# Rows of the source slots: from PSUM to their tile's partitions within SBUF, in two parts of sources, in a graph network's three convolutions

## The chip, the cores and the metric

The kernel runs on one core of a Trainium2 chip. The metric is the time of one execution in device microseconds. The engines are named as the profile names them: PE (TensorE matmul; PEld its weight loads), DVE (VectorE), ACT (ScalarE), POOL (GpSimd), SP (SyncE, which only issues DMAs here). Sixteen DMA engines serve all queues; q1 is the queue of the DMAs that SP issues, q0 that of the gathers that POOL issues.

## The reference

A graph of 12500 nodes (128 features each) and 200000 edges, sorted by destination. The first layer is an attention over each node's incoming edges; the change hardly touches it. The second layer is three graph convolutions, each followed by a batch norm:

```python
def _gcn_norm(edge_index, n):
    loop = arange(n)
    src, dst = concat([edge_index[0], loop]), concat([edge_index[1], loop])
    deg = segment_sum(ones_like(dst), dst, n)
    dinv = rsqrt(deg)
    return src, dst, dinv[src] * dinv[dst]

def _gcn_conv(x, W, b):
    h = x @ W
    return segment_sum(h[src] * norm[:, None], dst, n) + b

h = _batch_norm(relu(_gcn_conv(x, W1, b1)), g1, beta1)     # 128 -> 256
h = _batch_norm(relu(_gcn_conv(h, W2, b2)), g2, beta2)     # 256 -> 128
h = _batch_norm(_gcn_conv(h, W3, b3), g3, beta3)           # 128 -> 128
```

All is in float32. On average 16 edges end at a node.

## The kernel before

**Tiles and slots.** Destinations are cut into 106 tiles of TN = 118 nodes, sources into NS = 98 groups of P = 128 nodes. For every tile and every source group there are SB = 13 slots, each of which holds one edge or none; a tile thus has SL = 98 x 13 = 1274 slots. Edges that find no slot (there are 19.3 per tile and group on average) are overflow, up to OV = 768 per tile in JO = 6 columns of 128. The slot lists are made once, by a sort on DVE that runs beside the attention (`place_edges`): gi_d in DRAM holds, for every slot, the source's number within its group (uint8), dlS in SBUF the destination's number within the tile, srcO the overflow's source rows. If the overflow doesn't fit, another path (`conv_rows`) is taken; with these inputs the slots' path (`conv_slots`) is.

**One convolution.** The table t_d (12544 rows of 512 B in DRAM) holds the transformed features, and hs the same in SBUF, as 98 groups of 128 rows. Tiles go in NBK = 12 blocks of TB = 9.

- `take(b, m)` fetches the slots' rows of a block: for seven stretches of SG = 14 source groups it loads gi (one list, broadcast to 128 partitions), DVE compares it with the partition's number (go, L1221, a one-hot matrix, four groups at a time), PE multiplies go with hs (gp, L1224: 117 slot rows of one group, 9 tiles x 13), ACT copies four groups from PSUM to stage (L1226), and SP writes stage to the DRAM tile m (L1228), in 112 and 5 partitions, 7168 B each.
- `reduce(b, m)` sums by tile: POOL gathers the overflow's rows from t_d (rows, L148, six DMAs of 128 rows), SP reads the tile's 1274 slot rows back from m as mr (L1245, RC = 10 rows per partition, 5120 B), DVE makes the one-hots of the destinations (oh, L1249, 16 columns of 118), and PE adds up in zp: the tile's own rows tg with the identity (L1159), ten matmuls of mr (L1253), six of rows (L1255). After GN = 3 tiles, `finish` multiplies by dinv (db, L1163), and `use` applies bias and relu on ACT.

The rows of take(b) are issued between the tiles of reduce(b - 1); the order on each engine is set by the Tile framework's scheduler from this program order, and tiles rotate over bufs buffers (gi 3, go 3, stage 2, mr 3, rows 5, oh 2; gp and zp two each in PSUM). Every engine, and SP as the queue of DMA issues, runs its instructions in order.

**Between convolutions.** The results stay in big (SBUF, 128 x 12544 float32); the first convolution has 256 outputs, and its second half goes to DRAM as hb_d. `transform` multiplies them with the next weights into hs and t_d.

The profile counts two matmul records for one float32 matmul.

## Time and profile before

| | us |
|---|---|
| median of three runs (lowest, highest) | 6156.63 (6151.24, 6157.75) |
| the profiled execution, its own time | 6154.56 |
| its span | 6152.8 |
| busy: PE / PEld / DVE / ACT / POOL | 4406.0 / 4115.5 / 3396.2 / 1011.7 / 4084.2 |
| attention and sort, from the start | 0 to 2957 |
| first convolution | 3008 to 4028 |
| transform | 4028 to 4091 |
| second convolution | 4091 to 5072 |
| transform | 5072 to 5113 |
| third convolution | 5113 to 6093 |
| last stage and end | 6093 to 6153 |

The stages' bounds are the first and the last matmul of a stage. A group of the profile has line, engine, operation, out<-in by the program's names, and how often it ran, then busy us and the mean ns of one, then the engine's idle time just before it and what ended most of that. L12 is line 12 of the kernel. "DMA share" is the busy share of the 16 DMA engines, "PEclk" the clock granted to PE.

### The profile page before, as it was taken

What the parts mean: (1) busy time and instruction counts of PE and PEld (TensorE: products, weight loads), DVE (VectorE), ACT (ScalarE), POOL (GpSimd) and SP (SyncE); (2) the same over time, 40 slices, a digit from 0 to 9 for tenths busy, and PEclk for the clock granted to TensorE, in tenths of its full rate; (3) what the DMA queues carried; (4) which work ended last, traced back from release to release, by engine and by line L of the source; (5) the groups of instructions that cost most, each with busy time, mean ns of one, the idle gap of its engine ahead of it and who ended that gap; (6) DMA issues with size and microseconds to landing.
All of it is one profiled execution on the core that took longest, in us unless ns stands there. A gap on an engine that the chain in (4) does not pass through costs nothing. (4 is left out here: it accounts for less than half of the span.)

```text
span 6152.8 us, 80384 instructions
## 1 busy us (share of the span) xinstructions
PE 4406.0 (72%) x28564; PEld 4115.5 (67%) x28564; DVE 3396.2 (55%) x5972; ACT 1011.7 (16%) x2374; POOL 4084.2 (66%) x3617
## 2 busy tenths in 40 slices
PE   6676666666666665767487787877787787778777
PEld 2666655555566665666377777777777776777777
DVE  7566688887876677655243343353343344434344
ACT  3111111110111111111112122111121211112120
POOL 0777788888888888777266566636666664666663
PEclk9677766666676776767788888898888888888888
DMA  6555544433444444454588888878888887888888
GB/s 188 152 143 138 137 112 106 113 103 109 105 128 120 122 112 112 131 132 114 150 214 216 218 216 218 213 209 217 219 216 221 213 211 204 219 219 219 221 215 209
DMA packets 607714, 1051.07 MB, mean 171 GB/s; under 512 B 191227, under 2 KB 418491, under 8 KB 607201
## 3 DMA queue, kind: packets, MB, share of 16 engines
q1 hardware_dynamic: 464311, 695.85, 41.5%
q0 software_dynamic: 142608, 348.39, 23.9%
q8 instruction: 232, 3.80, 0.3%
q14 instruction: 175, 1.43, 0.1%
q10 hardware_dynamic: 388, 1.60, 0.1%
HBM read 773.19 MB, written 272.26 MB: 170 GB/s over the span
## 5 line engine op out<-in xcount | busy, mean ns | idle before, releaser
L148 POOL DMA_INDIRECT rows<-t_d,srcO x1908 | 1827.6, 958 | 1329.2 <-issue 560.2
L148 POOL DMA_INDIRECT kv<-kv_d,srcA x1696 | 2252.3, 1328 | 536.7 <-issue 484.3
L1249 DVE TENSOR_TENSOR oh<-nums,dlS 128x1888 f32<-128x1888 f32 x318 | 674.3, 2121 | 1527.2 <-PE zp L1255 1517.9
L1253 PE MATMUL zp<-oh,mr 128*128 128x118 f32 x6360 | 966.6, 319 | 567.5 <-DMA mr<-m 440.4
L1253 PEld LDWEIGHTS zp<-oh,mr 128*128 128x128 f32 x6360 | 925.5, 233 | 586.4 <-DMA mr<-m 348.7
L1019 PE MATMUL qe<-qt,oht 128*128 128x128 f32 x3392 | 841.4, 415 | 247.3 <-DVE kv L1020 110.7
L1224 PE MATMUL gp<-hs,go 128*117 128x128 f32 x7056 | 891.8, 281 | 125.8 <-DVE go L1221 69.8
L1019 PEld LDWEIGHTS qe<-qt,oht 128*128 128x128 f32 x3392 | 767.1, 310 | 289.7 <-issue 166.8
L1224 PEld LDWEIGHTS gp<-hs,go 128*117 128x117 f32 x7056 | 831.9, 184 | 165.1 <-issue 117.1
L1226 ACT COPY stage<-gp 117x512 f32<-117x512 f32 x1008 | 521.8, 532 | 1375.0 <-PE gp L1224 936.8
L1020 DVE TENSOR_TENSOR kv<-qe,kv 128x512 f32<-128x512 f32 x424 | 289.4, 685 | 678.8 <-DMA kv<-kv_d,srcA 536.8
L1089 PE MATMUL acc<-vals,oh 128*118 128x137 f32 x3392 | 539.8, 329 | 150.5 <-DVE vals L1082 150.0
L1089 PEld LDWEIGHTS acc<-vals,oh 128*118 128x118 f32 x3392 | 522.1, 225 | 171.6 <-DVE vals L1082 171.3
L1221 DVE TENSOR_SCALAR go<-gi,iota_q 128x468 f32<-128x468 uint8 x1008 | 427.8, 456 | 224.5 <-DMA gi<-gi_d 111.8
L1255 PE MATMUL zp<-oh,rows 128*128 128x118 f32 x3816 | 513.2, 288 | 0.2 <-DMA rows<-t_d,srcO 0.2
L1255 PEld LDWEIGHTS zp<-oh,rows 128*128 128x128 f32 x3816 | 492.2, 206 | 0.4 <-DMA rows<-t_d,srcO 0.4
L1058 PE MATMUL ends<-ident,mg 128*8 128x128 f32 x212 | 53.0, 343 | 344.4 <-DVE mg L1053 305.6
L1082 DVE TENSOR_TENSOR vals<-kv,vals 128x2048 f32<-128x2048 f32 x106 | 242.3, 2286 | 27.2 <-ACT vals L1081 26.8
L1058 PEld LDWEIGHTS ends<-ident,mg 128*8 128x8 f32 x212 | 11.7, 96 | 366.1 <-DVE mg L1053 298.8
L1023 DVE TENSOR_REDUCE sc<-kv 128x128 f32<-128x2048 f32 x106 | 240.8, 2272 | 0.0
L677 DVE TENSOR_TENSOR oh<-iota_f,dlA 128x1888 f32<-128x1888 f32 x106 | 224.0, 2113 | 5.0 <-PE acc L1089 5.0
L1036 PE MATMUL sm<-wbd,et 128*128 128x32 f32 x848 | 167.8, 351 | 45.0 <-DVE mg L1075 37.7
(242 smaller groups left out, 3648.1 us busy)
## 6 DMA issues: line engine op xcount, KB each, us to landing
m<-stage SPq DMA_DIRECT2D x252, 784.0 KB
mr<-m SPq DMA_DIRECT2D x318, 560.0 KB
dw_b<-dlb_d SPq DMA_DIRECT2D x106, 512.0 KB
gi<-gi_d SPq DMA_DIRECT2D x252, 204.8 KB
rows<-t_d,srcO POOLq DMA_INDIRECT x1908
kv<-kv_d,srcA POOLq DMA_INDIRECT x1696
ebx<-in_edge_attr_dram SPq DMA_DIRECT2D x106, 256.0 KB
mr<-m SPq DMA_DIRECT2D x318, 75.0 KB
```

The lines of the kernel that those rows point to most:

```text
L148: nc.gpsimd.indirect_dma_start(out=o, out_offset=None, in_=table[:, :], in_offset=bass.IndirectOffsetOnAxis(ap=idx, axis=0))
L1019: nc.tensor.matmul(qe[:, k, :], ohv[:, :, j + k], qt, start=True, stop=True)
L1020: nc.vector.tensor_tensor(qk[:, j:j + 4, :], qe, qk[:, j:j + 4, :], op=ALU.mult)
L1023: nc.vector.tensor_reduce(sc.rearrange("p h j -> p j h"), qk.rearrange("p j (h c) -> p j h c", h=H), AX.X, ALU.add)
L1082: nc.vector.tensor_tensor(vh[:, :, :, :C], kv[:, :, D:].rearrange("p j (h c) -> p j h c", h=H), vh[:, :, :, C:].to_broadcast([P, JJ, H, C] ...
L1089: nc.tensor.matmul(acc, oh[:, j, :], va[:, j, :], start=(j == 0), stop=(j == JJ - 1))
L1221: nc.vector.tensor_scalar(go[:, :n], gv[:, a:a + n], iota_q, None, op0=ALU.is_equal)
L1224: nc.tensor.matmul(gp[:, i, :], go[:, i].rearrange("p t k -> p (t k)"), hs[:, g * SG + a + i, :], start=True, stop=True)
L1226: nc.scalar.copy(stage[:, a:a + n, :], gp[:, :n, :])
L1249: nc.vector.tensor_tensor(oh, nums.unsqueeze(1).to_broadcast(sh), dlS[:, t, :].unsqueeze(2).to_broadcast(sh), op=ALU.is_equal)
L1253: nc.tensor.matmul(zp[:, i, :], mr[:q, j, :], oh[:q, j, :], start=False, stop=False)
L1255: nc.tensor.matmul(zp[:, i, :], rows[:, j, :], oh[:, RC + j, :], start=False, stop=(j == JO - 1))
```

## The change

The slots' rows no longer pass through DRAM. A block has TB = 8 tiles with SB = 16 slots each, so that one matmul of go and hs yields 128 slot rows, ordered slot by slot (k, then the tile t). The destination tile mr in SBUF has the shape (128, 8 tiles, 7, 128), and SP copies stage to it by SBUF-to-SBUF DMAs: the row group (k, t) of stage goes to the partitions q x 16 + k, at tile t, for the seven (or six) source groups at once. A transfer reads 128 partitions and writes 16.

Because mr now holds a whole block, the sources are cut into two parts, 8 x 7 = 56 groups and 7 x 6 = 42 groups. `take(b, part, mr)` fills mr for one part in four batches of up to 14 groups (eight transfers of 458,752 B for part 0, seven of 393,216 B for part 1), between the tiles of the part before. The sums of a tile stay open over both parts: `add_first` adds part 0 (seven matmuls), `add_rest` own rows, part 1 (six) and overflow (four). A matmul with zeros opens the PSUM bank of four tiles, and `finish` comes after four tiles (NG = 4) in place of three. There are 14 blocks, and 512 overflow edges per tile in four columns. dlS is set to -1 first, since not all its places are written. go reads gi in the order slot, tile, so neighbouring elements stand a tile's slots apart.

Buffers: gi 2, go 3, stage 2, mr 2, rows 6, oh 2; in PSUM gp 2, zp 3, hq 2. big and the DRAM tile m are gone. The results of every convolution go to DRAM (h_d), and transform and the last stage read them from there. The lists gi_d are laid out by batch, eight DMAs per block.

```diff
 MG = 4
-SB = 13
-OV = 768
+SB = 16
+OV = 512
 JO = OV // P
 TB = P // SB
-GN = 3
-SG = 14
+CA, CB = 7, 6
 NOT = 1 << 23
...
+    NA = TB * CA
+    NQ = (NS - NA) // CB
+    assert NA + NQ * CB == NS and NQ <= TB
+    parts = [(0, CA, TB), (NA, CB, NQ)]
+    RC = CA + CB
+
+    batches = [[(0, q, 2) for q in range(0, TB, 2)], [(1, q, min(2, NQ - q)) for q in range(0, NQ, 2)]]
+    MB = 2 * CA
...
-    gi_d = dram.tile([NBK, NS // SG, TB, SG * SB], U8, name="gi_d")
-    hb_d = dram.tile([P, NP], FP, name="hb_d")
+    gi_d = dram.tile([NBK, TB * SL], U8, name="gi_d")
+    h_d = [dram.tile([P, NP], FP, name=f"h{i}_d") for i in range(2)]
...
+        def batch(b, part, q, m):
+            s0, n, _ = parts[part]
+            s0, n = s0 + q * n, n * m
+            return s0, n, gi_d[b, TB * SB * s0:TB * SB * (s0 + n)].rearrange("(t k) -> t k", t=TB)
...
             for b in range(NBK):
                 tn = min(TB, NTT - b * TB)
-                nc.sync.dma_start(gi_d[b, :, :tn, :].rearrange("g t k -> t g k"),
-                                  sl[b * TB:b * TB + tn, :].rearrange("t (g k) -> t g k", g=NS // SG))
-            if NTT % TB:
-                none = rt.tile([NS // SG, (TB - NTT % TB) * SG * SB], U8, name="none")
-                yield
-                nc.vector.memset(none, 255)
-                nc.sync.dma_start(gi_d[NBK - 1, :, NTT % TB:, :].rearrange("g t k -> g (t k)"), none)
+                for x in batches[0] + batches[1]:
+                    s0, n, gi = batch(b, *x)
+                    nc.sync.dma_start(gi[:tn], sl[b * TB:b * TB + tn, s0 * SB:(s0 + n) * SB])
...
+                gy, gx, sg, mt, ga, ohs, wk = (pool(n, b) for n, b in (("gy", 2), ("gx", 3), ("sg", 2), ("mt", 2),
+                                                                         ("ga", 6), ("ohs", 2), ("wk", 2)))
...
-                def take(b, m):
-                    for g in range(NS // SG):
-                        stage = sg.tile([TS, SG, D], FP, name="stage")
-                        gi = gy.tile([P, TB, SG * SB], U8, name="gi")
-                        nc.sync.dma_start(gi.rearrange("p t k -> p (t k)"),
-                                          gi_d[b, g].rearrange("t k -> (t k)").unsqueeze(0)
-                                          .to_broadcast([P, TS * SG]))
-                        gv = gi.rearrange("p t (s k) -> p s t k", k=SB)
-                        for a, n in groups(SG, 4):
-                            go = gx.tile([P, 4, TB, SB], FP, name="go")
-                            nc.vector.tensor_scalar(go[:, :n], gv[:, a:a + n], iota_q, None, op0=ALU.is_equal)
-                            gp = ps.tile([TS, 4, D], FP, name="gp")
-                            for i in range(n):
-                                nc.tensor.matmul(gp[:, i, :], go[:, i].rearrange("p t k -> p (t k)"),
-                                                 hs[:, g * SG + a + i, :], start=True, stop=True)
-                            nc.scalar.copy(stage[:, a:a + n, :], gp[:, :n, :])
-                        for x, y in ((0, 112), (112, TS)):
-                            nc.sync.dma_start(m[x:y, g * SG:(g + 1) * SG, :], stage[x:y])
...
+                def ones_at(dl):
+                    oh = ohs.tile([P, CB + JO, TN], FP, name="oh")
+                    sh = [P, dl.shape[1], TN]
+                    nc.vector.tensor_tensor(oh[:, :sh[1]], nums.unsqueeze(1).to_broadcast(sh),
+                                            dl.unsqueeze(2).to_broadcast(sh), op=ALU.is_equal)
+                    return oh
+
+                def take(b, part, mr):
+                    n = parts[part][1]
+                    for _, q, m in batches[part]:
+                        s0, w, slots = batch(b, part, q, m)
+                        gi = gy.tile([P, P * MB], U8, name="gi")
+                        nc.sync.dma_start(gi[:, :P * w], slots.rearrange("t k -> (t k)").unsqueeze(0)
+                                          .to_broadcast([P, P * w]))
+                        gv = gi[:, :P * w].rearrange("p (t s k) -> p s k t", t=TB, k=SB)
+                        stage = sg.tile([P, MB, D], FP, name="stage")
+                        for a, c in groups(w, 4):
+                            go = gx.tile([P, 4, SB, TB], FP, name="go")
+                            nc.vector.tensor_scalar(go[:, :c], gv[:, a:a + c], iota_q, None, op0=ALU.is_equal)
+                            gp = pg.tile([P, 4, D], FP, name="gp")
+                            for i in range(c):
+                                nc.tensor.matmul(gp[:, i, :], go[:, i].rearrange("p k t -> p (k t)"),
+                                                 hs[:, s0 + a + i, :], start=True, stop=True)
+                            nc.scalar.copy(stage[:, a:a + c, :], gp[:, :c, :])
+                        for i in range(m):
+                            nc.sync.dma_start(mr[(q + i) * SB:(q + i + 1) * SB, :, :n, :],
+                                              stage[:, i * n:(i + 1) * n, :])
                         yield
 
-                def reduce(b, m):
-                    for t0 in range(b * TB, min(NTT, (b + 1) * TB), GN):
-                        n = min(GN, NTT - t0)
-                        zp = ps.tile([P, GN, TN], FP, name="zp")
-
-                        def add(i):
-                            t = t0 + i
+                zps = {}
+
+                def add_first(b, mr):
+                    for t in range(b * TB, min(NTT, (b + 1) * TB)):
+                        if t % NG == 0:
+                            zps[t // NG] = pz.tile([P, NG, TN], FP, name="zp")
+                            nc.tensor.matmul(zps[t // NG].rearrange("p a b -> p (a b)"), zero[:, :P], zero,
+                                             start=True, stop=False)
+                        zp = zps[t // NG][:, t % NG, :]
+                        oh = ones_at(dlS[:, t, :CA])
+                        for j in range(CA):
+                            nc.tensor.matmul(zp, mr[:, t % TB, j, :], oh[:, j, :], start=False, stop=False)
+                        yield
+
+                def add_rest(b, mr):
+                    K = NQ * SB
+                    for t0 in range(b * TB, min(NTT, (b + 1) * TB), NG):
+                        n = min(NG, NTT - t0)
+                        tg = own_rows(wk, table, t0, n)
+                        for t in range(t0, t0 + n):
+                            zp = zps[t // NG][:, t % NG, :]
                             rows = ga.tile([P, JO, D], FP, name="rows")
                             for j in range(JO):
                                 gather(rows[:, j, :], table, srcO[:, t, j:j + 1])
-                            k = (t - b * TB) * SB
-                            mv = m[k:k + SB].rearrange("k s d -> (k s) d")
-                            mr = mt.tile([P, RC, D], FP, name="mr")
-                            for x, y, r in ((0, 112, RC), (112, LP, RC), (LP, LP + 1, LR)):
-                                nc.sync.dma_start(mr[x:y, :r], mv[x * RC:(y - 1) * RC + r]
-                                                  .rearrange("(p c) d -> p c d", c=r))
-                            oh = wk.tile([P, RC + JO, TN], FP, name="oh")
-                            sh = list(oh.shape)
-                            nc.vector.tensor_tensor(oh, nums.unsqueeze(1).to_broadcast(sh),
-                                                    dlS[:, t, :].unsqueeze(2).to_broadcast(sh), op=ALU.is_equal)
-                            for j in range(RC):
-                                q = LP + (j < LR)
-                                nc.tensor.matmul(zp[:, i, :], mr[:q, j, :], oh[:q, j, :], start=False, stop=False)
+                            oh = ones_at(dlS[:, t, CA:])
+                            nc.tensor.matmul(zp, tg[:, t - t0, :], ident[:TN, :TN], start=False, stop=False)
+                            for j in range(CB):
+                                nc.tensor.matmul(zp, mr[:K, t % TB, j, :], oh[:K, j, :], start=False, stop=False)
                             for j in range(JO):
-                                nc.tensor.matmul(zp[:, i, :], rows[:, j, :], oh[:, RC + j, :], start=False,
-                                                 stop=(j == JO - 1))
-
-                        yield from finish(wk, table, t0, n, zp, use, ps, add)
-
-                taken = None
-                for b in range(NBK + 1):
-                    tiles = reduce(b - 1, taken) if b else iter(())
-                    if b < NBK:
-                        taken = blocks.tile([TS, NS, D], FP, name="m")
+                                nc.tensor.matmul(zp, rows[:, j, :], oh[:, CB + j, :], start=False,
+                                                 stop=(j == JO - 1 and t == t0 + n - 1))
+                            yield
+                        finish(wk, t0, n, zps.pop(t0 // NG), use, ph)
+                tiles = iter(())
+                for b in range(NBK):
+                    for part in range(2):
+                        mr = mt.tile([P, TB, CA, D], FP, name="mr")
                         done = 0
-                        for g, _ in enumerate(take(b, taken)):
-                            while done < g * TB * SG // (NS - SG):
+                        for g, _ in enumerate(take(b, part, mr)):
+                            while done < g * TB // (len(batches[part]) - 1):
                                 next(tiles, None)
                                 done += 1
-                    for _ in tiles:
-                        pass
-
-        def stats(st, h, t0, n):
-            w = min(n * TN, N - t0 * TN)
-            nc.vector.bn_stats(st[:, t0 // GN, :], h[:, :w])
+                        for _ in tiles:
+                            pass
+                        tiles = add_rest(b, mr) if part else add_first(b, mr)
+                for _ in tiles:
+                    pass
+
+        def result(wk, t0, n, z, func, bias, st, to):
+
+            h = wk.tile([P, NG * TN], FP, name="h")
+            nc.scalar.activation(h[:, :n * TN], z, func, bias=bias)
+            nc.vector.bn_stats(st[:, t0 // NG, :], h[:, :min(n * TN, N - t0 * TN)])
+            nc.sync.dma_start(to[:, t0 * TN:(t0 + n) * TN], h[:, :n * TN])
...
+        def load_h(sr, h, s0, n):
+            hb = sr.tile([P, NG * P], FP, name="hb")
+            nc.sync.dma_start(hb[:, :n * P], h[:, s0 * P:(s0 + n) * P])
+            return hb
```

## The prediction

> **What bounds the kernel now.** I read the shares of the span first, then the table by stage, then inside one convolution the queues, the costliest groups, the DMA issues and the waits. The page:
>
> ```profile
> PE 4406.0 (72%) x28564; PEld 4115.5 (67%) x28564; DVE 3396.2 (55%) x5972; ACT 1011.7 (16%) x2374; POOL 4084.2 (66%) x3617
> DMA  6555544433444444454588888878888887888888
> ```
>
> No engine is full over the span; the DMA row (busy tenths of the 16 engines, 40 slices) steps from 4 to 8 in the second half, where the change lies. By stage (stretch, us, busy us and records of PE, PEld, DVE, ACT, POOL, granted clock, DMA share, GB/s), the three convolutions:
>
> ```profile
> 3008.00:4028.00 1020.00, 805.78 (x6096) 776.03 (x6096) 402.19 (x543) 211.04 (x406) 586.68 (x614) 0.88 0.81 214
> 4091.00:5072.00 981.00, 770.95 (x5952) 752.41 (x5952) 383.88 (x511) 191.49 (x372) 608.34 (x635) 0.88 0.84 216
> 5113.00:6093.00 980.00, 768.22 (x5952) 750.21 (x5952) 382.77 (x510) 191.25 (x371) 609.17 (x635) 0.88 0.85 217
> ```
>
> 2981 of 6153 us. DMA is busiest (0.84), PE next (0.79); DVE, ACT and POOL have room. Inside the second one (4200 to 5000), the queues with packets, MB and share of the engines:
>
> ```profile
> q1 hardware_dynamic: 48215, 138.70, 64.3%
> q0 software_dynamic: 16696, 34.24, 19.8%
> ```
> SP's queue (q1) takes three times what the gathers (q0) do. In the same stretch, PE's longest wait and SP's (us in total, times, longest):
>
> ```profile
> PE zp L1253 <- DMA mr<-m: 134.2, 24, 8.5
> ```
> ```profile
> SPq L1228 <- ACT stage L1226: 392.3, 68, 9.5
> ```
>
> PE waits for rows read back from DRAM; SP stands before the writes to m until ACT has copied a batch, with whatever is next on its queue behind it. So the convolutions are bound by DMA, with PE close behind. The groups concerned (count | busy us, mean ns | idle before, releaser) and DMA issues, for all three convolutions:
>
> ```profile
> L148 POOL DMA_INDIRECT rows<-t_d,srcO x1908 | 1827.6, 958 | 1329.2 <-issue 560.2
> L1253 PE MATMUL zp<-oh,mr 128*128 128x118 f32 x6360 | 966.6, 319 | 567.5 <-DMA mr<-m 440.4
> L1224 PE MATMUL gp<-hs,go 128*117 128x128 f32 x7056 | 891.8, 281 | 125.8 <-DVE go L1221 69.8
> L1226 ACT COPY stage<-gp 117x512 f32<-117x512 f32 x1008 | 521.8, 532 | 1375.0 <-PE gp L1224 936.8
> L1221 DVE TENSOR_SCALAR go<-gi,iota_q 128x468 f32<-128x468 uint8 x1008 | 427.8, 456 | 224.5 <-DMA gi<-gi_d 111.8
> ...
> m<-stage SPq DMA_DIRECT2D x252, 784.0 KB
> mr<-m SPq DMA_DIRECT2D x318, 560.0 KB
> ...
> gi<-gi_d SPq DMA_DIRECT2D x252, 204.8 KB
> ```
>
> **What the Trainium skill says.** "SBUF — State Buffer", Door 1: DMA rate depends on how many of 16 ports the partitions reach; partitions 0 to 15 reach four and were measured at 104 GB/s, all 128 at 328. "DMA: Bandwidth & Descriptors", How many engines: the slowest dimensions of both sides (here 128 and 16) give the engine count, so 16, one destination partition each; and, under Back-pressure (written of transfers between cores), stalled writes stall the engine's other queues. The trace of before has no sizable write into few partitions to confirm this. SBUF's specification table: each step to a new 16-byte line costs; L866 agrees, 1274 elements read 52 bytes apart taking 2352 ns where a contiguous copy of as many (L862) takes 818:
>
> ```profile
> L866 DVE CAST A<-T x1: 2352/2352/2352, 2478.0 to 2478.0; 106x1274 f32<-106x1274 int32 x1
> ```
>
> **The change, part by part** (per convolution).
>
> *DMA removed.* 84 writes to m and 106 reads of mr. The trace's packet records from 3300 to 4000 us give 7168 B in 351 ns, 5120 B in 307, 1638 B in 115, gathers' 4096 B in 281, 512 B in 38, 1416 B in 86 (means). Over 16 engines: 84 x 117 x 0.351/16 = 216 us, 106 x 127 x 0.307/16 = 258 us. Of 636 gathers 212 go: each 16 packets, 0.28 us, so 59 us of DMA, and 212 x 0.958 = 203 us of POOL, which was not the bound. In sum 533 us of ring time off.
>
> *DMA added.* 14 blocks x (8 transfers of 458,752 B + 7 of 393,216 B), each into 16 partitions. At the skill's 104 GB/s, an estimate: 4.41 and 3.78 us, 61.8 us per block, 865 us. At full rate (the 7168 B packets' median 278 ns is 25.8 GB/s per engine, 413 for 16) it would be 218 us: those are the two ends. I take the low rate, since neighbouring transfers of a batch stand on the same rings in order, each engine with one partition.
>
> *DMA sum.* Before: 216 + 258 + gi 84 x 0.92 = 77 + gathers 179 + own rows 30 + db 25 = 785, 80% of 981 (the view says 84%). After: 865 + gi 22.5 MB at the same rate 99 + gathers 424 x 0.28 = 119 + 30 + 25 + h stores 27 x 0.92 = 25, **1163 us**. The ring alone is longer than the convolution now.
>
> *PE.* Before 1176 gathers by matmul + 106 x 17 = 2978 matmuls, 770.95/2978 = 0.259 us. After 1372 + 106 x 18 + 27 zeroing ones = 3307, 856 us, if the granted clock stays at 0.88: a floor under the ring.
>
> *How PE meets the ring.* Sums need every transfer of a part. In the built order, every second block has, after 88 matmuls of tiles without a gather between, 40 gathers and then the first sum of part 0, whose last four transfers start within those 40: the first 14 gathers 3.6 us, ACT's copy 0.6, the transfers 17.6, landing 2 (the skill's fixed cost of a DMA, same page, Anatomy), 23.8 us against 10.4 of PE: it waits some 13 us, and in like manner at part 1. With two mr and two stage buffers, ACT's copies wait for the transfers; SP stands at the next transfer for ACT, and the gi loads behind it on SP feed DVE's go and PE. So the ring also idles at times. I take it 90% full (784/981 was 80% when PE was nearly as long; here it is a third longer than PE): 1163/0.9 = 1292 us, ends 1163 and 1454.
>
> *DVE, ACT, SP.* go is 175,616 elements, now read at a stride of a tile's slots: at L866's 1.85 ns 325 us for 143, at most; one-hots in two parts 106 x (0.95 + 1.33) = 242 for 225. Sum about 585 of 1292, covered by the ring; if that cover were gone, four gathers' go (0.95 us) would pace PE (1.04 us) evenly. ACT 378 copies x 0.586 = 222, covered. SP's issues fall from about 680 to 430.
>
> *Outside.* h goes through DRAM wholly: 6.4 MB more to read in each transform and the last stage; at 214 GB/s 30 us each if nothing hides it (63, 41 and 60 us long now), nothing if the DVE work of 38 to 45 us does; I take 35 in all, 0 to 90. Laying out the slot lists: 13 DMAs become 120, at about 0.34 us of SP each, 41 us, with the attention's loads queued behind them and two tiles of 24 us buffered: 15, 0 to 45. The sort's tail has 1568 columns for 1274, 512 overflow for 768: 73 us of rows x 0.23 less 7, 10 us of DVE beside gathers: 5, 0 to 10. Together 55, 0 to 145. The zeroing of dlS and pad is under 2 us.
>
> *Sum.* 3 x 1292 + 10 (second h of the first) - 2981 = +905, +55: 6154.6 + 960 = **7115** against the profiled execution (span 6152.8 and 1.8 around it), 2 us below the median of three; forecast 7115.
>
> **Rivals.**
> 1. *Port-bound ring*, as above: 7115, its own range 6154.6 + 518 = 6673 (ring full, nothing outside) to 6154.6 + 1391 + 145 = 7691. For: the byte counts and four ports. Against: no row of this kernel shows the port.
> 2. *Half-bound*: the two transfers of a batch lie on different ports and overlap, 208 GB/s: ring 1163 - 433 = 730, below PE's 856. Then each of the 28 parts costs PE the wait for its last transfers: ACT's copy 0.6, two or three of 2.2 us, 2 to landing, about 9: 856 + 28 x 9 = 1108, so 6154.6 + 343 + 10 + 55 = 6560. For: a batch's two parts do start 16 partitions apart. Against: on one ring an engine writes them in order.
> 3. *No port limit, the order decides*: ring 516, and the same wait is 0.6 + 2 x 1.1 + 2 + the next gi behind them, about 6: 856 + 28 x 6 = 1024, so 6154.6 + 91 + 10 + 55 = 6310.
> 4. *Faster*, no port limit and the waits hidden: before, PE was 0.79 busy and waited 134 of 800 us for mr, 0.96 without; taken 0.94 busy, 856/0.94 = 910, so 6154.6 - 251 + 35 = 5940. It decides if the 16-partition transfers run above about 300 GB/s and a part's last one lands within the 12 to 40 gathers ahead of its first sum. For: the bytes moved fall from about 207 to 165 MB, and PE's floor of 856 lies under 981. Against: the port table, and 11% more matmuls.
> That the other path is run instead is excluded: counted from the inputs, the fullest tile has 736 overflow edges of 768 allowed before, 476 of 512 after.
>
> **How the numbers follow.** Case 1 0.70, case 2 0.12, case 3 0.07, case 4 0.10, no difference 0.01. Case 1 is likeliest, so the forecast is its time. The range 6270 to 7500 takes in 2 and 3, leaving out case 4 and the top of case 1. Measurements tell 0.2% (12 us) apart: faster 0.10, same 0.02, slower 0.88.
>
> **What would show it.** Right: convolutions of 1160 to 1450 us, DMA share over 0.9 with GB/s falling to about 130, packets of 3584 B at 400 to 600 ns instead of the 139 that 25.8 GB/s gives, PE and ACT waiting for mr and stage transfers. Wrong: such packets near 139 ns, PE over 0.85 busy, convolutions under 980 us; or the time lost outside them.

## The result, and the profile after

The changed kernel takes 7333.84 us (median of four runs, 7330.77 to 7363.26) against 6157.19 us for the kernel before on the same chip: **1.192 times as long, with a 95% interval of 1.188 to 1.195**. The forecast was 7115 us. The profiled execution took 7363.26 us, its span 7361.5, 1208.7 us more than before.

The runs below went to several chips, and on three of them the kernel before itself takes 7244 to 7387 us in place of 6157 to 6174; so a time is only set beside times of its own chip.

First the page of the kernel after, engine shares and the DMA row (tenths of a slice, 40 slices):

```profile
PE 4793.0 (65%) x30420; PEld 4451.7 (60%) x30420; DVE 3794.3 (52%) x6357; ACT 1081.4 (15%) x2464; POOL 3511.1 (48%) x2981
DMA  5555434444544354688888876888888788888888
```

PE is less busy in share and still no engine is full; DMA is again at 8 in the second half, which is longer now. The table by stage says where (stretch, us, busy us and records of PE, PEld, DVE, ACT, POOL, granted clock, DMA share, GB/s): convolution, transform, convolution, transform, convolution, last stage.

```profile
3040.00:4390.00 1350.00, 914.19 (x6688) 865.91 (x6688) 532.11 (x666) 231.51 (x430) 390.19 (x402) 0.82 0.83 123
4390.00:4529.00 139.00, 81.94 (x406) 73.99 (x404) 42.62 (x81) 1.26 (x4) 1.77 (x2) 0.68 0.47 146
4529.00:5875.00 1346.00, 878.16 (x6582) 851.28 (x6583) 514.64 (x640) 215.74 (x404) 410.44 (x423) 0.81 0.83 119
5875.00:5939.00 64.00, 38.10 (x208) 34.51 (x207) 39.81 (x70) 0.69 (x2) 1.97 (x2) 0.75 0.74 214
5939.00:7281.00 1342.00, 876.95 (x6583) 849.79 (x6583) 514.36 (x639) 216.09 (x404) 410.95 (x423) 0.80 0.83 120
7281.00:7361.00 80.00, 41.62 (x202) 37.42 (x200) 36.75 (x66) 0.69 (x2) 0.00 (x0) 0.66 0.77 224
```

The convolutions' 4038 us are 1057 more than the 2981 of before. The rest is 152: the attention and sort end 32 later, the transforms and the last stage take 283 for 164. The DMA share in the convolutions is as before, 0.83, while the GB/s fall from 216 to 119: the same engines are as long busy per microsecond with little more than half the bytes. In the middle of the second convolution (4700 to 5700) the queues are (packets, MB, share of 16 engines):

```profile
q1 hardware_dynamic: 49907, 97.58, 70.8%
q0 software_dynamic: 10240, 20.99, 11.8%
```

In 4529 to 5875 the trace's packet records give 3584 B in a median of 540 ns (mean 485), 3072 B in 461 (428). The groups and DMA issues of the three convolutions (count | busy us, mean ns | idle before, releaser):

```profile
L153 POOL DMA_INDIRECT rows<-t_d,srcO x1272 | 1236.1, 972 | 3023.6 <-PE zp L1284 1336.5
...
L1251 PE MATMUL gp<-hs,go 128*128 128x128 f32 x8232 | 1236.6, 317 | 777.0 <-DVE go L1248 428.0
...
L1248 DVE TENSOR_SCALAR go<-gi,iota_q 128x512 f32<-128x512 uint8 x1134 | 709.9, 656 | 1142.3 <-DMA gi<-gi_d 655.1
...
L1270 PE MATMUL zp<-oh,mr 128*128 128x118 f32 x4452 | 586.5, 299 | 312.6 <-DMA mr<-stage 178.0
...
L1286 PE MATMUL zp<-oh,mr 112*128 112x118 f32 x3816 | 506.8, 281 | 316.3 <-DMA mr<-stage 316.3
...
mr<-stage SPq DMA_DIRECT2D x336, 448.0 KB
mr<-stage SPq DMA_DIRECT2D x294, 384.0 KB
```

A third of the gathers and all of m's traffic are gone, as meant, and PE waits for the copies within SBUF in place of the reads from DRAM. The waits of SP and of PE in the second convolution (us in total, times, longest):

```profile
SPq L1255 <- ACT stage L1253: 562.3, 196, 21.2
SPq L1242 <- DMA gi<-gi_d: 216.6, 27, 15.9
SPq L1242 <- DVE go L1248: 162.6, 42, 11.5
```

```profile
PE gp L1251 <- DVE go L1248: 138.4, 39, 16.7
PE gp L1251 <- ACT stage L1253: 115.2, 41, 8.7
PE zp L1286 <- DMA mr<-stage: 104.9, 7, 15.2
PE zp L1270 <- DMA mr<-stage: 57.8, 7, 10.1
PE zp L1270 <- issue: 50.6, 7, 9.3
```

These five make 467 of the 468 us in which PE idles there (1346 - 878). The sums of part 0 (L1270) wait once in each of the 14 blocks, 7.7 us on average; for half of these waits the view names no releaser ("issue"). In all 21 waits of the sums PE starts 1.1 to 2.8 us after the last packet of a copy into mr has ended, so all of them, 213 us, are put down to the copies. The matmuls of gp wait for ACT and for go, and both of these wait in turn (same stretch):

```profile
ACT stage L1253 <- DMA mr<-stage: 229.3, 29, 10.7
DVE go L1248 <- DMA gi<-gi_d: 229.3, 30, 24.1
```

ACT waits for a stage buffer that copies still read, and DVE for a list whose load SP issues behind the copies of the batch before. So all five rows lead to the copies, those for go by way of the order on SP's queue.

### The profile page after: what moved, and what is told of

Read it like the earlier page. It is cut to its first block, busy times and chain, and to the rows that moved or that the text cites. A ratio compares the mean times of both kernels' runs of the same rounds, so it can differ in the third digit from the quotient of the medians.

```text
span 7361.5 us, 84103 instructions
## 1 busy us (share of the span) xinstructions
PE 4793.0 (65%) x30420; PEld 4451.7 (60%) x30420; DVE 3794.3 (52%) x6357; ACT 1081.4 (15%) x2464; POOL 3511.1 (48%) x2981
## 5 line engine op out<-in xcount | busy, mean ns | idle before, releaser
L153 POOL DMA_INDIRECT rows<-t_d,srcO x1272 | 1236.1, 972 | 3023.6 <-PE zp L1284 1336.5
L1251 PE MATMUL gp<-hs,go 128*128 128x128 f32 x8232 | 1236.6, 317 | 777.0 <-DVE go L1248 428.0
L1251 PEld LDWEIGHTS gp<-hs,go 128*128 128x128 f32 x8232 | 1176.1, 227 | 849.7 <-issue 428.7
L1233 DVE TENSOR_TENSOR oh<-nums,dlS 128x826 f32<-128x826 f32 (+1 forms) x636 | 763.3, 1201 | 1156.7 <-PE zp L1270 873.6
L1248 DVE TENSOR_SCALAR go<-gi,iota_q 128x512 f32<-128x512 uint8 x1134 | 709.9, 656 | 1142.3 <-DMA gi<-gi_d 655.1
L1253 ACT COPY stage<-gp 128x512 f32<-128x512 f32 x1134 | 595.4, 548 | 2816.6 <-PE gp L1251 1961.8
L1270 PE MATMUL zp<-oh,mr 128*128 128x118 f32 x4452 | 586.5, 299 | 312.6 <-DMA mr<-stage 178.0
L1270 PEld LDWEIGHTS zp<-oh,mr 128*128 128x128 f32 x4452 | 578.4, 215 | 321.8 <-issue 257.3
L1286 PE MATMUL zp<-oh,mr 112*128 112x118 f32 x3816 | 506.8, 281 | 316.3 <-DMA mr<-stage 316.3
L1286 PEld LDWEIGHTS zp<-oh,mr 112*128 112x128 f32 x3816 | 472.8, 197 | 325.1 <-issue 278.7
```

Source lines behind the costliest of these rows:

```text
L153: nc.gpsimd.indirect_dma_start(out=o, out_offset=None, in_=table[:, :], in_offset=bass.IndirectOffsetOnAxis(ap=idx, axis=0))
L1233: nc.vector.tensor_tensor(oh[:, :sh[1]], nums.unsqueeze(1).to_broadcast(sh), dl.unsqueeze(2).to_broadcast(sh), op=ALU.is_equal)
L1248: nc.vector.tensor_scalar(go[:, :c], gv[:, a:a + c], iota_q, None, op0=ALU.is_equal)
L1251: nc.tensor.matmul(gp[:, i, :], go[:, i].rearrange("p k t -> p (k t)"), hs[:, s0 + a + i, :], start=True, stop=True)
L1253: nc.scalar.copy(stage[:, a:a + c, :], gp[:, :c, :])
L1270: nc.tensor.matmul(zp, mr[:, t % TB, j, :], oh[:, j, :], start=False, stop=False)
```

## The experiments

Three theories. **A**: the write ports of 16 neighbouring partitions set the pace of the copies, the copies that of the ring, the ring that of the convolution. **B**: a copy within SBUF is slow as such. **C**: what counts is the order on SP's queue (copies, lists and stores behind each other), whatever a copy costs.

### On a first chip: the control, the ports, the bytes, the buffers

Here the kernel before takes 6174.09 us. The control is the kernel after, unchanged.

> The changed kernel itself, beside edits of it on one chip, since absolute times of different chips are not to be set against each other. All theories: the ratio to the kernel before that was measured first, 1.19, with convolutions of some 1345 us and the 3584-byte packets at a median of 540 ns. If the ratio on this chip is another one, the ratios of the edits are read against it.

7352.55 us, ratio 1.191 (1.188 to 1.194), as first measured. Its convolutions take 1351, 1337 and 1331 us, its 3584-byte packets a median of 539 ns.

**Copies spread over the partitions.** A transfer's 16 target partitions lie 8 apart (part 0) or 7 apart (part 1), not side by side. By the Trainium skill, "SBUF — State Buffer", Door 1, whose rule gives each partition its port, those 16 reach 8 ports (part 0) and 14 or 15 (part 1) in place of 4.

```diff
-                            nc.sync.dma_start(mr[(q + i) * SB:(q + i + 1) * SB, :, :n, :],
+                            nc.sync.dma_start(mr[q + i:(SB - 1) * parts[part][2] + q + i + 1:parts[part][2], :, :n, :],
```

(The destinations' numbers dlS are laid out in the same order, by one changed view.)

> The same copies to the gathered tile, but each landing in 16 partitions that lie 8 (first part) or 7 (second part) apart, in place of 16 neighbours. Theory A (the write ports of 16 neighbouring partitions set the pace of the ring, and the ring that of the convolutions): packets at about half, 3584 bytes at 280 ns and 3072 bytes at 200 ns, ring filled to about 0.5, and convolutions at least 200 us shorter each, so about 0.90 of the changed kernel's time. Theory B (a copy within SBUF is slow whatever it lands on): packets and time unchanged. Theory C (the order of the copies, loads and stores on one queue sets the pace, whatever a copy costs): packets halved, time within 3% of the changed kernel's.

6661.90 us, ratio 1.079 (1.077 to 1.080): 691 us less, 0.906 of the control. The second convolution of the control and of this kernel, as in the table by stage:

```profile
4540.00:5877.00 1337.00, 872.16 (x6584) 845.06 (x6584) 514.11 (x640) 215.80 (x404) 410.95 (x422) 0.81 0.83 119
```

```profile
4295.00:5404.00 1109.00, 856.03 (x6584) 828.19 (x6584) 515.31 (x640) 215.96 (x404) 410.03 (x423) 0.88 0.61 144
```

The same records of each engine, the same bytes, 228 us less. The packets of 3584 B have a median of 282 ns, those of 3072 B 188: 1.9 and 2.4 times as fast for 2 and at least 3.5 times the ports. So B falls, since it is the same copy, and that the place of the target partitions sets its pace is shown; that the ports are the reason rests on the page, and the three rates (106, 203 and 261 GB/s over 16 engines at 4, 8 and 14 or 15 ports) rise with its counts. PE's waits, in the control and then with the spread copies:

```profile
PE gp L1251 <- DVE go L1248: 137.9, 38, 19.3
PE gp L1251 <- ACT stage L1253: 118.0, 43, 9.0
PE zp L1286 <- DMA mr<-stage: 106.1, 7, 15.8
PE zp L1270 <- DMA mr<-stage: 55.1, 7, 10.2
PE zp L1270 <- issue: 46.4, 7, 8.7
```

```profile
PE gp L1251 <- DVE go L1248: 121.1, 43, 9.5
PE gp L1251 <- ACT stage L1253: 46.8, 35, 3.3
PE zp L1286 <- DMA mr<-stage: 28.7, 5, 5.9
PE zp L1270 <- issue: 22.0, 7, 3.7
PE zp L1270 <- DMA mr<-stage: 21.0, 7, 4.7
PE zp L1286 <- issue: 12.1, 2, 6.2
```

Counting the "issue" rows, the waits for mr fall from 207.6 us by 124, those for stage by 71, those for go by 17 only: together the 212 us of PE's idle time that went; the other 16 are PE's busy time, 856 us for 872, at a granted clock of 0.88 for 0.81. The ring is no longer the bound here: it is filled to 0.61 (A said about 0.5). What is left looks like hand-offs: a copy's time still stands between ACT and the next list, and between the last batch of a part and its first sum. Which of them counts was not tested on this chip.

**Fewer bytes in the same copies.** Each copy, still into 16 neighbours, carries two of its seven or six columns. (mr is then two fixed tiles, one for each part, zeroed at the start of a convolution, in place of two that rotate; this part of the edit is not shown.)

```diff
-                            nc.sync.dma_start(mr[(q + i) * SB:(q + i + 1) * SB, :, :n, :],
-                                              stage[:, i * n:(i + 1) * n, :])
+                            nc.sync.dma_start(mr[(q + i) * SB:(q + i + 1) * SB, :, :2, :],
+                                              stage[:, i * n:i * n + 2, :])
```

> The same number of copies in the same order, but each carries 2 of the 7 or 6 groups of columns, 1024 bytes per packet; the sums then read two groups of fresh data and otherwise zeros. Theory A: the copies cost under a third, and the convolutions fall to what PE's own work and the hand-offs leave, about 1000 to 1090 us each, 0.85 to 0.88 of the changed kernel's time. Theory B: the same fall, if the cost goes by bytes; if it goes by the copy, no change. Theory C: convolutions stay within 5% of 1345 us.

5879.61 us, ratio 0.952 (0.951 to 0.954). Second convolution and PE's longest waits in it:

```profile
4050.00:4889.00 839.00, 785.63 (x6583) 766.26 (x6583) 505.55 (x639) 215.75 (x404) 407.89 (x422) 0.97 0.52 116
```

```profile
PE gp L1251 <- DVE go L1248: 38.6, 27, 6.8
PE zp L1286 <- DMA mr<-stage: 8.9, 7, 3.3
```

All of PE's, DVE's, ACT's and POOL's work is there, in the same order on SP's queue, and the convolution takes 839 us, below the 980 of before. So C falls as a cause by itself: PE idles only 53 us (839 - 786) in the same order once a copy is short. It also shows what the change would bring if its copies cost little; it is no version of the kernel, since most columns are missing.

A's numbers missed too: 839 us for 1000 to 1090, and 0.80 of the control's time for 0.85 to 0.88. One reason is that the copies shrank by more than their bytes. Packets of 1024 B take a mean of 77 ns (median 49), so all copies of the second convolution take 129 us of the ring for the control's 764, a sixth, where the bytes are 0.31. That is 214 GB/s over 16 engines into the same 16 neighbours, where the 3584-byte packets have 106 by their median and 119 by their mean (482 ns): neither is a fixed rate of such a target. Why short packets go faster was not tested.

**Six buffers in place of three for the loads of h** (and for what rotates with them in the transforms).

```diff
-                sr = s.enter_context(tc.tile_pool(name="sr", bufs=3))
+                sr = s.enter_context(tc.tile_pool(name="sr", bufs=6))
```

> The buffers of h, of the evicted first sums and of the loads of the transforms doubled from three to six, everything else the same. If the 76 us that the first transform gained are the latency of its h loads with three buffers, the transform falls from 139 to about 75 us and the kernel by about 80 to 100 us (0.985 to 0.99 of the changed kernel's time), with convolutions unchanged. If the copies at the end of the convolution hold it up, it stays at about 139 us.

7286.49 us, ratio 1.181 (1.179 to 1.183), 66 us less than the control, a little short of the 80 to 100 expected. In the control's first transform PE does 16 matmul records per step and waits for a load each time (start, us, engine and group, idle before):

```profile
4443.81 3.79 PE L1351 MATMUL tp<-wa,hb 128*128 128x128 f32 x16 [1.90 <-DMA hb<-h_d]
4449.53 2.05 PE L1351 MATMUL tp<-wa,hb 128*128 128x128 f32 x16 [1.94 <-DMA hb<-h_d]
```

A step of the first transform takes two loads, so three buffers hold one step and a half. With six, both transforms (by stage):

```profile
4386.00:4464.00 78.00, 55.71 (x410) 50.15 (x409) 43.18 (x82) 1.26 (x4) 1.89 (x2) 0.93 0.87 270
5797.00:5854.00 57.00, 32.73 (x202) 29.28 (x203) 38.08 (x70) 0.69 (x2) 2.06 (x2) 0.80 0.87 252
```

78 and 57 us for the control's 141 and 58; the convolutions keep their lengths (1333 and 1337 in the second). The time lost in the first transform was load latency with too few buffers, not bandwidth: its DMA share rises from 0.47 to 0.87.

### On a second chip: the same edits, and the lists on another queue

These runs were made before those on the first chip. Here the kernel before takes 7263.73 us; the times in the expectations were written for the chip of the result. The kernel with six buffers stands in for the kernel after, since its convolutions are the same program. The next three edits are those above.

> The changed kernel with one edit: a transfer from stage to mr writes 16 partitions that stand 8 apart (part 0) or 7 apart (part 1) in place of 16 neighbours; bytes, packets, order and queues are the same. By the skill's port table the 16 neighbours reach 4 ports, 8 apart reach 8 ports (two engines each), 7 apart 14 or 15. Theory A (the write ports set the pace): packets of 3584 B fall from a median of 520 ns to about 280, those of 3072 B from 432 to 120-200; the transfers' share of the ring falls from about 726 to 400 us per convolution, and a convolution from 1346 to 1050-1120 us; about 6500 us in all. Theory B (a copy within SBUF is slow as such, by its reads or its three-dimensional descriptors): packets stay at 520 and 432, and the time within 50 us of 7334. Theory C (the order of the instructions makes PE wait, not the ring): packets get shorter, but the convolutions lose less than 100 us each.

> The changed kernel, but each transfer moves 2 of its 7 (or 6) source groups; the other columns of mr are zeroed once and stay so. Left out: the slot rows of the other groups don't reach the sums. Instructions, queues and order are the same, the bytes 0.30 of before. Theory A (ring): the transfers' 726 us fall to about 265 at the same rate, the ring to about 660, under PE; convolutions of 980-1060 us, about 6350 in all. Theory C (order): with transfers as many and in the same order, convolutions stay above 1250 us.

> The changed kernel with 6 buffers for hb, og and x1 in place of 3 in the transforms and the last stage. In the first transform each step takes two hb of three buffers, so the next step's loads wait for this one's matmuls, some 5 us per step, 139 us in all (63 before). If that is its cause, the first transform falls to 65-90 us and the total by 50 to 75; if the bytes through DRAM are (6.4 MB more), it stays within 10 us.

Spread: 7459.87 us, ratio 1.026 (1.021 to 1.031). Fewer bytes: 6790.71 us, one run. Six buffers: 8108.60 us, ratio 1.113 (1.107 to 1.119). The second convolutions take 1337, 1086 and 1601 us: so spread copies take 264 us less than the last, and fewer bytes 515, where the first chip gave 228 and 498. So the absolute expectations missed and the differences repeat. Each of these convolutions is some 230 to 270 us longer here. In whole times the kernel before loses most, 1090 us, where they lose 798, 911 and 822; that makes their ratios smaller here. The traces put part of it down to "remote", an event without a recorded issuer, as with six buffers (all of the span):

```profile
DVE zt L1184 <- remote: 305.0, 40, 13.2
```

The control has no such wait. What sends them late was not found.

**The lists' loads issued by ACT**, so that they no longer stand behind the copies on SP:

```diff
-                        nc.sync.dma_start(gi[:, :P * w], slots.rearrange("t k -> (t k)").unsqueeze(0)
+                        nc.scalar.dma_start(gi[:, :P * w], slots.rearrange("t k -> (t k)").unsqueeze(0)
```

> The changed kernel with the loads of gi issued on ACT's queue and not SP's, so that they don't stand behind the transfers. DVE waited 655 us for gi in all. Theory A (ring): the bytes and packets stay, so the wait for gi turns into one for stage or mr; 7334 minus 0 to 120. Theory C (the order behind SP decides): most of the 655 us goes, 7334 minus 300 to 600, with packets of 3584 B still at 520 ns.

7683.38 us, ratio 1.057 (1.053 to 1.062). The second convolution takes 1383 us, 218 less than 1601, with the copies as slow as ever (3584 B at a median of 534 ns) and the ring at 0.82 in place of 0.69. PE's waits for go are all but gone, and those for ACT have grown, probably because ACT's own queue now stands before lists (the view names no releaser for 496 us of ACT's idle time):

```profile
PE gp L1251 <- ACT stage L1253: 308.7, 105, 10.0
...
PE gp L1251 <- DVE go L1248: 5.9, 3, 4.0
```

With six buffers on this chip the same two rows read 103.7 and 120.7 us. In all it is 425 us less than with six buffers: what C had forecast (300 to 600 less with the packets as slow), not A (0 to 120 less). So the place of the lists behind the copies counts too where the ring is only 0.69 full; either edit alone, spread copies or lists elsewhere, takes over 200 us from a convolution here. It brought the convolution back towards the ring's own time (1139 us here), not below it. On the first chip, where the ring is at 0.83 with the lists on SP, this was not run, and how the loss divides there between slow copies and lists behind them stays open.

### On two more chips: lists ahead, a straight read, and all together

**The list of a batch loaded one batch ahead**, on SP, before the copies of the batch before it:

```diff
+                order = iter([(b, part, q, m) for b in range(NBK) for part in range(2)
+                              for _, q, m in batches[part]])
+                ahead = []
+                def load():
+                    for args in order:
+                        s0, w, slots = batch(*args)
+                        gi = gy.tile([P, P * MB], U8, name="gi")
+                        nc.sync.dma_start(gi[:, :P * w], slots.rearrange("t k -> (t k)").unsqueeze(0)
+                                          .to_broadcast([P, P * w]))
+                        ahead.append((s0, w, gi))
+                        return
+                load()
                 def take(b, part, mr):
                     n = parts[part][1]
                     for _, q, m in batches[part]:
-                        s0, w, slots = batch(b, part, q, m)
-                        gi = gy.tile([P, P * MB], U8, name="gi")
-                        nc.sync.dma_start(gi[:, :P * w], slots.rearrange("t k -> (t k)").unsqueeze(0)
-                                          .to_broadcast([P, P * w]))
+                        load()
+                        s0, w, gi = ahead.pop(0)
```

> The list of a batch is loaded one batch ahead: its load stands on SyncE's queue before the copies of the batch before it, not after them; copies and ports as in the changed kernel. Theory A (the ports of 16 neighbouring partitions set the pace of the ring, at 540 ns per 3584 bytes): the ring's 1117 us per convolution stay as they are, and only its idle sixth can shrink; convolutions end at 1150 to 1300 us, ring filled to over 0.87, ratio to the kernel before 1.10 to 1.18. Theory C (the order on the queue alone sets the pace): convolutions near 1000 us, ratio near 1.03. Theory D (neither: VectorE's expansion and the sums wait on each other through the two tiles of gathered rows): no change, 1.19.

8036.78 us, ratio 1.087 (1.082 to 1.093), on a chip where the kernel before takes 7386.93. The second convolution takes 1522 us with a ring sum of 1112 us, filled to 0.73. The ring's work is unchanged, as A says, but the convolution, the fill and the ratio all lie outside A's ranges, and C's 1000 us did not come either. No unchanged kernel ran on this chip, and 1601 us is of another. The nearest is the next kernel below, the changed one but for the read of the list: its 8199.18 us in all and 1569 us in the second convolution are 162 and 47 us more than here. So loading ahead seems to gain some 2% there, unless the straight read costs time.

**The straight read of the list.** The expansion reads the bytes as they lie; the rows that it then picks are not those that the sums want. In the changed kernel neighbouring elements stand up to 224 bytes apart (14 groups of 16 slots), not 16 as the expectation says.

```diff
-                        gv = gi[:, :P * w].rearrange("p (t s k) -> p s k t", t=TB, k=SB)
+                        gv = gi[:, :P * w].rearrange("p (s k t) -> p s k t", t=TB, k=SB)
```

> The expansion reads the list in the order in which its bytes lie, in place of every 16th; the rows picked are then others than the sums want, at the same number of instructions and bytes. If the stride is what made the expansion 656 ns in place of 456: back to about 456 ns, 75 us less of VectorE per convolution. Theory A: the time stays within 0.5% of the changed kernel's, ratio 1.19, since VectorE is waited for only behind late lists. If VectorE's expansion is on the chain: up to 75 us per convolution less, ratio 1.155.

8199.18 us, ratio 1.112 (1.105 to 1.118), on the same chip. Of the group go, the form of four source groups in the second convolution, here and with six buffers (busy us, mean ns, idle before):

```profile
L1248 DVE TENSOR_SCALAR go<-gi,iota_q 128x512 f32<-128x512 uint8 x308 | 141.8, 488 | 402.5 <-DMA gi<-gi_d 222.4 <-PE gp L1251 156.0 <-remote 23.8
```

```profile
L1248 DVE TENSOR_SCALAR go<-gi,iota_q 128x512 f32<-128x512 uint8 x307 | 203.2, 695 | 358.0 <-DMA gi<-gi_d 208.8 <-PE gp L1251 130.3 <-remote 17.2
```

The stride costs 207 ns of 695 (691 in the kernel with the lists ahead, on the same chip), and DVE is 70 us less busy per convolution (444 for 514). What that is worth in time is without a control: the ratio, 1.112, is near neither 1.19 nor 1.155, which were written for another chip; the idle time before it is 45 us longer where go saves 61, which fits a DVE that is waiting anyway, but it is no proof.

**All three: spread copies, lists ahead, six buffers.**

> Three edits together: copies that land 8 or 7 partitions apart, the list loaded one batch ahead, and six buffers in place of three for h and the transforms' loads. If ports and order are what is left between the changed kernel and PE's own 840 us per convolution: convolutions at 860 to 980 us with the ring at 0.65 to 0.8, and 0.93 to 1.0 of the kernel before. If the order on the queue does not matter once the copies are cheap: convolutions stay near the 1110 us of the spread copies alone and the whole near 6590 us, 1.067 of the kernel before.

> The same three edits, once more, for a chip on which the kernel before takes its 6150 to 6180 us: there the spread copies alone gave 6662 us with convolutions of 1110 us and six buffers 66 us less than three. If the late list was what held the spread copies' convolutions above PE's 840 us: convolutions at 860 to 980 us, 5,850 to 6,250 us in all, 0.95 to 1.01 of the kernel before. If something else holds them: convolutions near 1110 us and 6590 us, 1.067. On a chip where the kernel before takes 7,200 us or more: 1.007 as measured.

7433.57 us, ratio 1.007 (1.003 to 1.010), beside the last two; and on one more chip 7365.32 us against 7243.50, ratio 1.017 (1.013 to 1.022). So it is 0.7% and 1.7% longer than the kernel before: no gain on either chip, though both differences are below 2%. Its second convolutions take 1334 and 1325 us, where spread copies alone took 1337 on the second chip, and its first transforms 79 and 76; neither the 860 to 980 us nor the 1110 us of the expectations came. The ratio is better than that of the spread copies alone, 1.026, by 1.9% and 0.9%, of which the transform explains some 0.8% (60 of 7300 us). As far as times of different chips can be set side by side, convolutions as long as with spread copies alone say that loading lists ahead brings little beyond. No complete version tried here beats the kernel before. On a chip like the first this one was not run, and there PE waited 121 us per convolution for go with spread copies; what it would bring is open.

## Why the prediction was right, and where it was off

**The side and the cause** held: slower, by a port-bound ring (rival 1). The packets of 3584 B took a median of 540 ns, within the 400 to 600 named; PE and ACT wait for mr and stage transfers; the convolutions lie at 1342 to 1350, within the 1160 to 1450. Spreading the copies' targets alone takes 691 of 1178 us away. The step that was argued with least evidence, the page's 104 GB/s for four ports, is borne out for these packets: 16 engines x 3584 B / 540 ns is 106 GB/s. It is no general rate, as the 1024-byte packets show. The 2 us for a transfer's landing came from a section on DMAs that POOL issues; for the copies, which SP issues, the trace has 1.1 to 2.8 us.

**The ring's sum** was 1163, measured 1118 (packet records of the second convolution). Term by term: the copies 770 for 865, since their mean is 485 ns, below the median: not all meet a full port; gi 104 for 99; gathers 150 for 119, since their 4096 B take a mean of 355 ns for 281; own rows, db and h about 65 for 80; packets of 4 bytes and instructions some 24 that were not counted.

**The fill of the ring** is the step that failed most: taken at 0.90, because the ring is a third longer than PE; measured 0.83, just under the 0.84 of before. 1118/0.90 would be 1242, and 1346 came, 104 us per convolution. A longer ring did not become fuller; by the waits, the same copies also delay what feeds it: SP stood 562 us before copies until ACT had a batch, ACT waited 229 us for its stage buffers, and DVE 229 us for lists behind copies. On the second chip, lists elsewhere raised the fill from 0.69 to 0.82. With the ring's sum 45 too long and its idle time too short, the convolution came out at 1292 for 1346, and three of them at +905 for +1057. That it came so near is partly luck: the long sum hid about half of the fill's error, and with the measured fill 1163 would have given 1401.

**PE's waits at the first sums**: some 13 us each in every second block. At part 1 that held: seven waits, 104.9 us in all, 15.0 each. At part 0 every block waits, fourteen times 7.7 us, 108.4 in all (57.8 + 50.6). So the total, 213 us for 14 x 13 = 182, was close, the picture of part 0 was not. That waits for go and stage would add 254 us more was said in words (ACT's copies wait, the lists stand behind SP) but got no term beside the fill.

**PE's floor** of 856 us at the clock of before, 0.88: with spread copies PE is busy 856.0 us at that clock. After, the clock was 0.81 and the busy time 878.

**Outside**, 55 was taken with an upper end of 145; 152 came. The front end, 20 for the lists and the sort, was 32. The transforms and the last stage, 35 (0 to 90), were 119. Of these, 76 lie in the first transform, where "at 214 GB/s 30 us each if nothing hides it" counted bytes and not the latency of two loads per step through three buffers; six buffers give 63 of them back.

**DVE**: go was put at 325 us per convolution at most; 237 came (709.9/3), and DVE is busy 515 for the 585 named. It stayed covered.

**The rivals.** Rival 2 put the convolution at 1108 us, with copies at 208 GB/s and hand-offs at every part; with spread copies, 3584 B in 282 ns, which is 203 GB/s over 16 engines, the second convolution took 1109. As a reading of the change it was wrong: the copies didn't run at that rate. As the answer to "and if a copy took half as long" its number came, largely by luck: it put 252 us of waits at the parts, and PE did idle 253 us, but 84 of them at mr and 121 at go. Rival 4, faster at 910 us, is where short copies lead (839), and its condition, transfers above some 300 GB/s, was not met by any placement of full copies tried. The DMA share of over 0.9 and the 130 GB/s that were to show the step right were 0.83 and 119: both are the fill again.

## What to carry to other kernels

Before a round trip by DRAM is replaced by copies within SBUF, count the ports that one transfer's target partitions reach: the DMA share alone (0.83 on both sides) doesn't tell a ring that moves bytes from one that waits on four ports, the GB/s beside it and the ns per packet do. A stride in the target partitions can be had for one changed view of the index, and took about two thirds of a convolution's loss away (228 of 357 us, on chips like that of the result). A ring that is on the path with two-deep buffers on both sides need not be full (0.83 here): take the fill that the kernel shows, and where a stage's data moves from SBUF to DRAM, count its loads per step against its buffers, not the bytes alone.

## What the runs showed of the hardware that was not expected

- The granted clock of PE went with its busy share: 0.81 with PE busy 65% of the convolution, 0.88 at 77%, 0.97 at 94% (after, spread, fewer bytes). PE's same matmuls took 878, 856 and 786 us, so less waiting and a shorter busy time came together; why the clock moved so was not tested.
- Into the same 16 neighbouring partitions, packets of 3584 B moved at 119 GB/s over 16 engines and packets of 1024 B at 214 (both by the mean, control and fewer bytes).
- The gathers' 4096-byte packets took a mean of 344 ns in the control and 309 beside spread copies on the first chip, but 321 beside both on the second. That copies into few ports slow other traffic on the ring is thus not shown.
- The kernel before took 6157 and 6174 us in two sets of runs and 7244 to 7387 on three other chips, and the traces that these left show waits of up to 10 us and more without a recorded releaser. A difference of one edit was about the same on both kinds (228 and 264 us, 498 and 515).
